# Windowed attention with sinks: both score tiles of a cycle in one run, and the overflow guard from Gram matrices of the weights

## The chip, the cores and the metric

The kernel runs on one core of one Trainium2 chip. The metric is the device time of the whole program in microseconds (us). Before the change three runs took 4219.34, 4223.46 and 4220.33 us; their median is 4220.33 us. The engines are called PE (TensorE, matmuls), PEld (TensorE's weight loads), DVE (VectorE), ACT (ScalarE), POOL (GpSimd) and SP (SyncE, which only starts DMAs here).

## What is computed

The program is a network of 16 stages on 4096 tokens of width 128 (16 sequences of 256). The change lies in one stage, an attention with sinks, whose reference is, cut to its core:

```python
x = rmsnorm(h, attn_norm_scale)
q = apply_interleaved_rope(einsum('bqm,muh->bquh', x, Wq) + bq, cos, sin) * SCALE   # 16 heads of 64
k = apply_interleaved_rope(einsum('bkm,mvh->bkvh', x, Wk) + bk, cos, sin) * SCALE   # 4 heads, SCALE = 64**-0.25
v = einsum('bkm,mvh->bkvh', x, Wv) + bv
scores = einsum('bquh,bkuh->buqk', q, repeat(k, 4))
scores = where(abs(pos[:, None] - pos[None, :]) <= 128, scores, -1e9)
probs = softmax(concatenate([scores, sink], -1))[..., :-1]
h = h + einsum('bquh,uhm->bqm', einsum('buqk,bkuh->bquh', probs, v), Wo) + bo
h = h + moe(rmsnorm(h, moe_norm_scale), ...)
```

The kernel takes the exponential of the scores without subtracting their maximum. So that no overflow can go unseen, it writes bounds into a tile `peaks` as it goes. After the network, `over` (L2759) takes, for each of seven places (`STAGES`, L42), the maximum of the first side times the maximum of the second and compares it with `LIMITS` (L43). If one is above its limit, a second, slower version of the whole network runs. With the inputs given it does not run.

## The kernel before

All activations stay in SBUF, features on the partitions and tokens along the free axis, in eight chunks (`NCH`) of 512 tokens (two sequences of 256). The stage `window` (L2448) holds two buffers of all tokens, `h` and `n1`, calls `window_attention` (L3190), and then the mixture of experts of the same block. It follows the stage `mix` (L2076); the weights of a stage (here `w<-in_window_f`) are loaded while the stage before it runs.

**Units.** The attention's work is cut into 128 units `(c, side, b, it, jt)`: chunk, side (heads 0 to 7 or 8 to 15), sequence in the chunk, tile of 128 queries, tile of 128 keys. Units `n` (even, `jt = 0`) and `n + 1` (odd, `jt = 1`) share their queries. For one unit:

- `score` (L3249): two matmuls of 64 rows of the array each, on the upper and the lower half of the partitions, each 64x128 keys against 512 columns (four heads by 128 queries), into two PSUM banks. ACT then takes the exponential of both into a tile `pt`.
- `masked` (L3262): where `it` and `jt` differ, DVE multiplies `pt` by the window's mask; on the odd unit POOL adds the two units' `pt` into `both`.
- `weigh` (L3272): matmuls with the values as weights, 32 columns each, into the bank `po`; on the odd unit also matmuls of ones with `both`, which give the sums, into the bank `pd`.
- `inverse` (L3296): ACT takes Ln of the sums with the sink added, then Exp of minus that. `divide` (L3304): DVE multiplies `po` by it.

The inputs come from `prepare` (L3226), for a chunk and side in four steps: projections of k and q (`roped`, L3207: one matmul and two DVE operations that read its bank), a shuffle on DVE and an add on POOL (`moved`, L3217), and the values. `before` (L3329) normalises a chunk in three steps: centring, spread, scaling. For chunk 0 its spread is a matmul with the matrix of means; for the later chunks it is the matmuls of L1798 (`compact_spread`), whose rows a DMA spreads out. `after` (L3341) does the second norm likewise. `out` (L3314) is the output projection.

**The order** is written out by hand (`manual_schedule`): each engine runs its instructions as the loop at L3354 emits them. In an even slot n: `score(n)`, then what is due (masks, inverses), then a step of `prepare`, `out`, `before` and `after`, whichever fall there. In an odd slot: `score(n)`, what is due (divides), then `weigh` of units n-3 and n-2. Two slots make a cycle; there are 64 cycles. The slots from -14 to -1 are the ramp: the norm of chunk 0 at -14, -12 and -10, its `prepare` at -8 to -2. Instructions outside the hand-written order (such as `es` and the peak of the sinks at the start of the stage) are placed by the language's scheduler, and may run inside the stage before.

**PSUM** has eight banks; four go by the tag "s" (scores, projections, norms, outputs) and four by "o" (`po` and `pd`, two of each in turn). A bank is used again in the order of the requests for its tag, once its last reader is done.

**The guard.** After each projection `peak` (L1666) takes, on DVE, the largest absolute value of the finished q or k (128x512): 80 of them in the stage. They are due four slots after their `prepare` step.

Of the kernel before, what the change touches and what calls it, by code (L numbers as in the profile page):

```python
# [11 lines left out]
F32, BF16, I32 = mybir.dt.float32, mybir.dt.bfloat16, mybir.dt.int32  # L12
SP = mybir.EngineType.SP
AF = mybir.ActivationFunctionType
ALU = mybir.AluOpType
AX = mybir.AxisListType

P = 128
B, T, C = 16, 256, 128
# [20 lines left out]
BOUND, LOW = 60.0, 38.0  # L40
PEAKS = 4 * NCH
STAGES = DECAY, ROPE, WINDOW, WINDOW1, SINKS, LOCAL_A, LOCAL_B = range(7)  # L42
LIMITS = (BOUND * 8**0.5 / 8, BOUND * 8**0.5 / 4, LOW / 64, LOW / 64, LOW, LOW / 8, LOW / 8)  # L43


class Pack:
# [40 lines left out]
def _rows(v, n=P):  # L87
    v = np.asarray(v)
    return np.broadcast_to(v.reshape(1, -1), (n, v.size))
# [7 lines left out]
def _consts(fast=False):  # L97
# [18 lines left out]
    p.add("ones4", _rows((i[None, :32] // 8 == np.arange(4)[:, None]).reshape(-1)))  # L116
    p.add("limits", [LIMITS[n] for n in STAGES])
    if not fast:
# [1531 lines left out]
class Fast(Net):  # L1650
# [1400 lines left out]
    def guard(self, stage, c, q, k):  # L3051
        self.peak(stage, 0, c, q)
        self.peak(stage, 1, c, k)
# [136 lines left out]
    def window_attention(self, w, h, n1, ns2):  # L3190


        nc = self.nc
        with ExitStack() as st:
            p1 = self.stage(st, "w1", 1)
# [6 lines left out]
            units = [(c, side, b, it, jt) for c in range(NCH) for side in range(2) for b in range(2) for it in range(2) for jt in range(2)]  # L3202
            qs, ks, vs, pts, ots, sums, both, due = {}, {}, {}, {}, {}, {}, {}, {}
# [3 lines left out]
            def roped(n, g, s, t1):  # L3207


                pa = self.bank("s")  # L3210
                self.mm(pa, w["W" + n][:, g * P : g * P + P], n1[:, s])
                t2 = p2.tile([P, CH], F32, tag="t2", name="t2", bufs=4)
                for t, table in ((t2, w["sin"]), (t1, w["cos"])):
                    self.stt(self.bt(t), self.bt(pa), w["b" + n][:, g : g + 1], self.twice(table), ALU.add, ALU.mult)
                pending.append((t1, t2))

            def moved():  # L3217
                t1, t2 = pending.pop(0)
                t3 = p2.tile([P, CH], F32, tag="t3", name="t3")
                nc.vector.stream_shuffle(t3, t2, [d ^ 1 for d in range(32)])  # L3220
                self.gt(t1, t1, t3, ALU.add)

            def later(slot, f, *args):
                due.setdefault(slot, []).append((f, args))

            def prepare(i, step, slot):  # L3226

                c, side = divmod(i, 2)
                s = self.chunk(c)
                while pending:  # L3230
                    moved()
                if step == 0:
                    qs[i] = p2.tile([P, 4, CH], F32, tag="q", name="q")
                    ks[i] = p2.tile([P, CH], F32, tag="k", name="k")
                    roped("k", side, s, ks[i])
                    later(("last", slot + 4), self.peak, WINDOW + side, 1, c, ks[i])
                for g in ((0,), (1, 2), (3,), ())[step]:
                    roped("q", 4 * side + g, s, qs[i][:, g])
                    later(("last", slot + 4), self.peak, WINDOW + side, 0, 4 * c + g, qs[i][:, g])
                if side == 0 and step > 1:  # L3240
                    pv = self.bank("s")
                    v = p1.tile([P, 2, T], F32, tag="v", name="v", bufs=4)
                    for k in range(2):
                        t = 2 * step - 4 + k
                        self.mm(pv[:, k * T : k * T + T], n1[:, c * CH + t * P : c * CH + t * P + P], w["Wv"])
                        vs[c, t] = v[:, k]
                    self.tt(v, self.bt(pv), w["bv"][:, None, :].broadcast_to([P, 2, T]), ALU.add)

            def score(n):  # L3249
                c, side, b, it, jt = units[n]  # L3250
                i0, j0 = b * T + it * P, b * T + jt * P
                q, k = qs[2 * c + side], ks[2 * c + side]
                pt = p2.tile([P, 2, 4, P], F32, tag="pt", name="pt", bufs=6)
                ps = [self.bank("s"), self.bank("s")]
                for half in range(2):
                    rows = slice(64 * half, 64 * half + 64)
                    self.mm(ps[half].rearrange("p (h t) -> p h t", h=4), k[rows, j0 : j0 + P], q[rows, :, i0 : i0 + P])
                for half in range(2):
                    self.act(pt[:, half].rearrange("p h t -> p (h t)"), ps[half], AF.Exp)
                pts[n] = pt  # L3260
# [11 lines left out]
            def weigh(n, slot):  # L3272
                c, side, b, it, jt = units[n]
                if jt == 0:
                    sums[0] = self.bank("o"), self.bank("o")
                pt = pts.pop(n)
                po, pd = sums[0]


                for dh in range(3 if jt else 2):  # L3280
                    if dh == 2:
                        pt = both.pop(n)
                    for r in range(4):
                        half, hh = divmod(r, 2)
                        d = (2 * side + half) * 64 + 32 * dh
                        at = dh % 2 * T
                        nc.tensor.matmul(
                            (pd if dh == 2 else po)[32 * r : 32 * r + 32, at : at + T],
                            self.ones64[:, :32] if dh == 2 else vs[c, 2 * b + jt][:, d : d + 32],
                            pt[:, half, 2 * hh : 2 * hh + 2].rearrange("p h t -> p (h t)"),  # L3290
                            start=dh == 2 or (jt == 0 and dh == 0), stop=dh == 2 or (jt == 1 and dh == 1), skip_group_check=True,
                        )
                if jt:
                    later(slot + 1, inverse, n, po, pd, slot + 2)
# [34 lines left out]
            def before(c, i):  # L3329

                s = self.chunk(c)
                if i == 0:
                    held["sq"] = self.centre_step(p1, self.x[:, s], h[:, s], "s", square=True)
                elif i == 1:
                    held["rs"] = self.spread_step(p1, held["sq"], "s", twice=True, compact=c > 0)
                else:
                    r1, r2 = held["rs"]
                    self.stt(n1[:, s], h[:, s], w["ns1"], r2, ALU.mult, ALU.mult)
                    self.tt(h[:, s], h[:, s], r1, ALU.mult)
# [9 lines left out]
                else:  # L3349
                    self.stt(n1[:, s], h[:, s], ns2, held["rs"], ALU.mult, ALU.mult)  # L3350

            with self.share(s=4, o=4), self.tc.manual_schedule():
                self.logs()
                for n in range(-14, len(units) + 16):  # L3354
                    if 0 <= n < len(units):
                        score(n)
                        later(n + 1, masked, n)
                    for f, args in (*due.pop(n, []), *due.pop(("last", n), [])):
                        f(*args)
                    if n % 2:  # L3360
                        for i in (n - 3, n - 2):
                            if 0 <= i < len(units):
                                weigh(i, n)
                        continue
                    i, step = divmod(n + 8, 8)
                    if 0 <= i < 2 * NCH:
                        prepare(i, step // 2, n)
                    i, rest = divmod(n - 14, 8)
                    if rest == 0 and 0 <= i < 2 * NCH:
                        out(i)  # L3370
                    c, u = divmod(n + 16, 16)
                    if c == 0 and u in (2, 4, 6):
                        before(c, u // 2 - 1)
                    if u in (0, 2, 6) and 0 < c < NCH:
                        before(c, (u + 1) // 3)
                    c, u = divmod(n - 24, 16)
                    if u in (0, 2, 6 if c < NCH - 1 else 4) and 0 <= c < NCH:
                        after(c, (u + 1) // 3 + (u == 4))
# [497 lines left out]
```

## Time and profile before

| what | value |
|---|---|
| median of three runs | 4220.33 us |
| the profiled execution | 4218.15 us |
| its span, first to last instruction | 4216.4 us |
| DVE, pt<-pt,w (mask), 128x1024 | 1.29 us each, one a cycle (2930 to 3300 us) |
| POOL, both<-pt, 128x1024 | 2.36 us each, one a cycle |
| ACT, pt<-ps (exponential), 128x512 | 0.60 us each, four a cycle |
| DVE, t<-ps,w and q<-ps,w (projection), 128x512 | 0.74 to 0.75 us each |
| DVE, peaks<-q, 128x1 from 128x512 | 0.68 us each, 64 in the stage |
| DVE, peaks<-k | 0.67 us each, 16 in the stage |

The profile is of one execution. A row names the engine, the line of the kernel (often a helper's: L504 is every `mm`, L528 every activation), the operation with the tiles that it writes and reads, and how often it stands there. Matmuls of 32-bit numbers appear as two instructions each. A shape such as 64*128 behind a matmul is the part of the array that it takes: rows of the array by columns. "idle before" is time in which the engine did nothing, with the engine and tile that ended it; "issue" is a wait for nothing that the profile shows. In the timeline several like instructions are merged into one row, xN. Since ends of matmuls are modelled, the distance from start to start is the safer reading.

### The profile page before, as it was taken

What the parts mean: (1) busy time and instruction counts of PE and PEld (TensorE: products, weight loads), DVE (VectorE), ACT (ScalarE), POOL (GpSimd) and SP (SyncE); (2) the same over time, 40 slices, a digit from 0 to 9 for tenths busy, and PEclk for the clock granted to TensorE, in tenths of its full rate; (3) what the DMA queues carried; (4) which work ended last, traced back from release to release, by engine and by line L of the source; (5) the groups of instructions that cost most, each with busy time, mean ns of one, the idle gap of its engine ahead of it and who ended that gap; (6) DMA issues with size and microseconds to landing.
All of it is one profiled execution on the core that took longest, in us unless ns stands there. A gap on an engine that the chain in (4) does not pass through costs nothing. (4 is left out here: it accounts for less than half of the span.)

```text
span 4216.4 us, 74153 instructions
## 1 busy us (share of the span) xinstructions
PE 3831.5 (91%) x29030; PEld 2182.7 (52%) x29030; DVE 2551.0 (61%) x4503; ACT 2281.8 (54%) x4478; POOL 1853.7 (44%) x1632
## 2 busy tenths in 40 slices
PE   7999999998899999985989869888999999899978
PEld 3555466464455466454965459543444344455333
DVE  4776576374577477473346633556877676486474
ACT  6665466555766466652457634444554454774532
POOL 4754365232565166225433434454555455321251
PEclk8999999998999999996999979999999999999979
DMA  1800000000000000004920058100000000000000
GB/s 61 347 15 12 11 9 9 22 1 1 20 11 14 6 7 9 6 11 142 323 69 12 17 182 295 41 19 21 16 14 16 8 0 10 7 2 19 6 0 21
DMA packets 110086, 190.88 MB, mean 45 GB/s; under 512 B 16126, under 2 KB 70788, under 8 KB 109600
## 3 DMA queue, kind: packets, MB, share of 16 engines
q1 hardware_dynamic: 97248, 162.83, 11.7%
q0 software_dynamic: 9120, 18.51, 1.3%
q8 instruction: 231, 3.78, 0.4%
q10 hardware_dynamic: 3360, 4.72, 0.3%
q14 instruction: 127, 1.04, 0.1%
HBM read 118.28 MB, written 54.20 MB: 41 GB/s over the span
## 5 line engine op out<-in xcount | busy, mean ns | idle before, releaser
L528 ACT ACTIVATE pt<-ps 128x512 f32<-128x512 f32 x640 | 339.5, 600 | 337.5 <-PE ps L504 336.2
L504 PE MATMUL ps<-hb,w 128*128 128x512 f32 (+1 forms) x960 | 463.7, 617 | 3.9 <-issue 3.3
L504 PE MATMUL ps<-w,hb 128*128 128x512 f32 (+2 forms) x896 | 405.2, 573 | 27.3 <-DVE t L531 18.5
L534 POOL TENSOR_TENSOR t<-t,t 128x512 f32<-128x512 f32 x256 | 319.9, 1271 | 153.7 <-DVE t L531 107.8
L531 DVE TENSOR_TENSOR t<-ps,tab 128x512 f32<-128x512 f32 x512 | 317.5, 681 | 70.1 <-ACT sq L528 66.7
L534 POOL TENSOR_TENSOR t<-t,ss 128x1024 f32<-128x1024 f32 x128 | 243.7, 1904 | 195.2 <-ACT ss L528 194.0
L504 PEld LDWEIGHTS ps<-hb,w 128*128 128x128 f32 (+1 forms) x960 | 179.6, 191 | 261.8 <-issue 220.6
L528 ACT ACTIVATE qkt<-ps 128x512 f32<-128x512 f32 x256 | 140.6, 595 | 299.2 <-PE ps L508 299.2
L531 DVE TENSOR_TENSOR u<-u,ps 128x384 f32<-128x384 f32 (+1 forms) x206 | 121.8, 595 | 277.2 <-ACT u L528 114.9
L534 POOL TENSOR_TENSOR nsq<-ha 128x512 f32<-128x512 f32 x112 | 123.2, 1100 | 354.3 <-ACT ha L528 342.3
L531 DVE TENSOR_TENSOR ot<-ps,rd 128x512 f32<-128x512 f32 (+2 forms) x224 | 143.2, 639 | 209.8 <-ACT rd L528 209.8
L504 PEld LDWEIGHTS ps<-w,hb 128*128 128x128 f32 x896 | 154.1, 193 | 174.4 <-issue 111.7
L534 POOL TENSOR_TENSOR both<-pt 128x1024 f32<-128x1024 f32 x64 | 151.2, 2363 | 199.0 <-DVE pt L531 191.3
L504 PE MATMUL ps<-ot,w 128*128 128x512 f32 x448 | 213.6, 611 | 17.4 <-DVE ot L531 9.9
L504 PE MATMUL ps<-xt,w 128*128 128x128 f32 x1704 | 221.0, 280 | 1.6 <-ACT xt L528 1.5
L2225 POOL DMA_INDIRECT back<-y,x x142 | 139.1, 980 | 186.1 <-ACT y L528 69.5
L504 PE MATMUL ps<-u,w 128*128 128x512 f32 (+1 forms) x448 | 215.4, 605 | 3.4 <-POOL u L534 3.4
L504 PEld LDWEIGHTS ps<-xt,w 128*128 128x128 f32 x1704 | 204.5, 194 | 3.4 <-ACT xt L528 3.4
L528 ACT ACTIVATE u<-ps,w 128x512 f32<-128x512 f32 x160 | 107.7, 685 | 173.3 <-PE ps L504 170.6
L3479 PE MATMUL ps<-qkt 64*128 64x192 f32 (+1 forms) x2048 | 181.8, 311 | 9.6 <-ACT rd L528 9.6
L504 PE MATMUL ps<-ha,w 128*128 128x512 f32 x320 | 176.1, 672 | 11.6 <-ACT f L528 10.2
L504 PE MATMUL ps<-nsq,ct 128*128 128x512 f32 x272 | 154.5, 652 | 30.8 <-POOL nsq L534 26.6
(366 smaller groups left out, 8756.2 us busy)
## 6 DMA issues: line engine op xcount, KB each, us to landing
w<-in_moe_x SPq DMA_DIRECT2D x142, 533.0 KB
rows<-t SPq DMA_DIRECT2D x64, 520.0 KB
nrs<-nrow SPq DMA_DIRECT2D x220, 64.0 KB
x<-rows SPq DMA_DIRECT2D x142, 65.0 KB
w<-in_local_f SPq DMA_DIRECT2D x8, 659.5 KB
y<-back ACTq DMA_DIRECT2D x16, 256.0 KB
y<-back SPq DMA_DIRECT2D x16, 256.0 KB
w<-in_local_f SPq DMA_DIRECT2D x4, 658.5 KB
```

The costliest lines, as they stand in the source:

```text
L504: self.nc.tensor.matmul(out, lhsT, rhs, start=start, stop=stop)
L528: self.nc.scalar.activation(out, in_, func, **kw)
L531: self.nc.vector.tensor_tensor(out, a, b, op)
L534: self.nc.gpsimd.tensor_tensor(out, a, b, op)
L2225: nc.gpsimd.indirect_dma_start(views[i], bass.IndirectOffsetOnAxis(ap=x[:, C : C + 1].bitcast(I32), axis=0), y, None, bounds_check=2 * NT ...
L3479: nc.tensor.matmul(out, kt[rows, g, t * P : t * P + P], qt[rows, g, t * P : t * P + wide], start=(i, t) == (0, 0), stop=i == 1, skip_group ...
```

## The change

Three things are changed in `window_attention`.

1. In the order: `score(n)` and `score(n + 1)` are both emitted in the even slot n, one after the other, and both units' masks are due at n + 2 (before: n + 1 and n + 2). Weighing, inverses and divides keep their slots.
2. The banks: five for "s", two for "o" (`po`), and one with a tag of its own, "d", for `pd`.
3. The guard: the peaks of q and k are gone. Instead POOL makes copies of Wq and Wk scaled by the square of the norm's weights, and twice in the ramp (slots -14 and -12, behind the first and the second step of the norm of chunk 0) a function `guard` makes, for one side, five Gram matrices W^T diag(ns1^2) W of 128x128 and five products of a bias with itself, reduces the rows' absolute sums on DVE, and writes a bound of the squared length of q and k into `peaks`. The limits of both places become (38 x 8)^2, since the bounds are squares.

```diff
@@ -40,7 +40,7 @@
 BOUND, LOW = 60.0, 38.0
 PEAKS = 4 * NCH
 STAGES = DECAY, ROPE, WINDOW, WINDOW1, SINKS, LOCAL_A, LOCAL_B = range(7)
-LIMITS = (BOUND * 8**0.5 / 8, BOUND * 8**0.5 / 4, LOW / 64, LOW / 64, LOW, LOW / 8, LOW / 8)
+LIMITS = (BOUND * 8**0.5 / 8, BOUND * 8**0.5 / 4, (LOW * 8) ** 2, (LOW * 8) ** 2, LOW, LOW / 8, LOW / 8)
 
 
 class Pack:
@@ -3223,6 +3223,30 @@
             def later(slot, f, *args):
                 due.setdefault(slot, []).append((f, args))
 
+            scaled = [p1.tile([P, w["W" + n].shape[1]], F32, tag="s" + n, name="scaled") for n in "qk"]
+            for t, n in zip(scaled, "qk"):
+                nc.gpsimd.tensor_scalar(t, w["W" + n], w["ns1"], w["ns1"], ALU.mult, ALU.mult)
+
+            def guard(side):
+
+                pg, pb = self.bank("s"), self.bank("s")
+                for i in range(5):
+                    k, g = (1, side) if i == 4 else (0, 4 * side + i)
+                    at = slice(g * P, g * P + P)
+                    gram = pb[:, P:T] if k else pg[:, i * P : i * P + P]
+                    self.mm(gram, w["W" + "qk"[k]][:, at], scaled[k][:, at])
+                    b = w["b" + "qk"[k]][:, g : g + 1]
+                    self.mm(pb[:, i : i + 1], b.broadcast_to([P, P]), b)
+                r = p1.tile([P, 5], F32, tag="bound", name="bound")
+                reduce = nc.vector.tensor_reduce
+                reduce(r[:, :4], pg.rearrange("p (m d) -> p m d", d=P), AX.X, ALU.add, apply_absolute_value=True)
+                reduce(r[:, 4:], pb[:, P:T], AX.X, ALU.add, apply_absolute_value=True)
+                self.ts(r, r, P * 16.0 / 15.0, ALU.mult)
+                for k, some in enumerate((slice(0, 4), slice(4, 5))):
+                    at = ((WINDOW + side) * 2 + k) * PEAKS
+                    peaks = self.peaks[:, at : at + some.stop - some.start]
+                    self.stt(peaks, pb[:, some], 16.0, r[:, some], ALU.mult, ALU.add)
+
             def prepare(i, step, slot):
 
                 c, side = divmod(i, 2)
@@ -3233,10 +3257,8 @@
                     qs[i] = p2.tile([P, 4, CH], F32, tag="q", name="q")
                     ks[i] = p2.tile([P, CH], F32, tag="k", name="k")
                     roped("k", side, s, ks[i])
-                    later(("last", slot + 4), self.peak, WINDOW + side, 1, c, ks[i])
                 for g in ((0,), (1, 2), (3,), ())[step]:
                     roped("q", 4 * side + g, s, qs[i][:, g])
-                    later(("last", slot + 4), self.peak, WINDOW + side, 0, 4 * c + g, qs[i][:, g])
                 if side == 0 and step > 1:
                     pv = self.bank("s")
                     v = p1.tile([P, 2, T], F32, tag="v", name="v", bufs=4)
@@ -3272,7 +3294,7 @@
             def weigh(n, slot):
                 c, side, b, it, jt = units[n]
                 if jt == 0:
-                    sums[0] = self.bank("o"), self.bank("o")
+                    sums[0] = self.bank("o"), self.bank("d")
                 pt = pts.pop(n)
                 po, pd = sums[0]
 
@@ -3349,12 +3371,13 @@
                 else:
                     self.stt(n1[:, s], h[:, s], ns2, held["rs"], ALU.mult, ALU.mult)
 
-            with self.share(s=4, o=4), self.tc.manual_schedule():
+            with self.share(s=5, o=2, d=1), self.tc.manual_schedule():
                 self.logs()
                 for n in range(-14, len(units) + 16):
-                    if 0 <= n < len(units):
-                        score(n)
-                        later(n + 1, masked, n)
+                    if n % 2 == 0 and 0 <= n < len(units):
+                        for i in (n, n + 1):
+                            score(i)
+                            later(n + 2, masked, i)
                     for f, args in (*due.pop(n, []), *due.pop(("last", n), [])):
                         f(*args)
                     if n % 2:
@@ -3371,6 +3394,8 @@
                     c, u = divmod(n + 16, 16)
                     if c == 0 and u in (2, 4, 6):
                         before(c, u // 2 - 1)
+                        if u < 6:
+                            guard(u // 2 - 1)
                     if u in (0, 2, 6) and 0 < c < NCH:
                         before(c, (u + 1) // 3)
                     c, u = divmod(n - 24, 16)
```

## The prediction

> **What bounds the kernel now.** I read the page first, then the stage's stretches, then TensorE's timeline in it. The page gives the times and the busiest engine:
>
> ```profile
> span 4216.4 us, 74153 instructions
> PE 3831.5 (91%) x29030; PEld 2182.7 (52%) x29030; DVE 2551.0 (61%) x4503; ACT 2281.8 (54%) x4478; POOL 1853.7 (44%) x1632
> L504 PE MATMUL ps<-xt,w 128*128 128x128 f32 x1704 | 221.0, 280 | 1.6 <-ACT xt L528 1.5
> ```
>
> A share over 16 stages says little about one, so here is this stage by stretches: ramp, ramp, steady work. The columns are the stretch, its length, busy time (instructions) of PE, PEld, DVE, ACT and POOL, the granted clock, and DMA.
>
> ```profile
> 2872.00:2886.00 14.00, 8.58 (x11) 3.12 (x12) 3.81 (x6) 6.42 (x10) 2.15 (x2) 0.67 0.34 119
> 2898.00:2904.00 6.00, 5.41 (x8) 2.02 (x9) 1.97 (x3) 1.09 (x2) 0.54 (x1) 0.50 0.00 0
> 2915.00:3345.00 430.00, 426.88 (x3449) 176.41 (x3448) 341.11 (x539) 214.99 (x491) 240.52 (x138) 1.00 0.06 14
> ```
>
> TensorE is busy 426.88 of 430 us at full clock; DVE has 79%, ACT 50%, POOL 56%. So in the steady part only what shortens TensorE's queue counts, and in the ramp TensorE is not the bound. Two views of TensorE's timeline (start, length, operation):
>
> ```profile
> 3310.62 1.13 PE L504 MATMUL ps<-q,k 64*128 64x512 f32 x4
> 3311.68 3.70 PE L504 MATMUL ps<-ot,w 128*128 128x512 f32 x8
> 3315.31 1.13 PE L504 MATMUL ps<-q,k 64*128 64x512 f32 x4
> 3316.37 1.93 PE L3287 MATMUL ps<-pt,v 128*32 128x256 f32 x32
> 3318.12 0.61 PE L3287 MATMUL ps<-both,ct 128*32 128x256 f32 x8
> 3318.67 1.99 PE L504 MATMUL ps<-q,k 64*128 64x512 f32 x8
> 3320.58 0.64 PE L3287 MATMUL ps<-pt,v 128*32 128x256 f32 x8
> ```
>
> ```profile
> 3103.15 0.43 PE L1798 MATMUL ps<-nsq,ct 128*32 128x128 f32 x8
> 3103.51 1.68 PE L504 MATMUL ps<-q,k 64*128 64x512 f32 x4
> 3105.11 1.93 PE L3287 MATMUL ps<-pt,v 128*32 128x256 f32 x32
> ```
>
> A matmul is two instructions. One cycle (two units) is: scores S, whole-array work P (projections, out), scores S, weighted values and sums W. I read start to start. S alone takes 1.06 (3310.62 to 3311.68, and 3315.31 to 3316.37). Where a cycle has no P, both scores already stand together (x8) and take 1.91, not 2.12. So being split costs 0.20. In the second view, behind the row sums of a norm (R, L1798), S takes 1.60, 0.54 over its 1.06.
>
> **The change, part by part.**
>
> *Both scores in one run.* 64 cycles; in three the scores are together already. 61 x 0.20 = 12.3 us off. All of it is on TensorE's queue, which sets the end.
>
> *The wait behind R.* There are 13 such S; start to start they take 20.0 us where 13 x 1.06 = 13.8. The second half of S waits for one of the four "s" banks, which holds a projection that DVE copies out at 3103.07 to 3103.81. In the new order S stands ahead of the projections and R ahead of W, which takes "o" and "d" banks. When S next needs the projection's bank, all of W (2.3 us) and half of S have passed. Off: 6.2 us. R and W also share the 128*32 shape: a group of sums takes 0.55 where another shape follows (3318.12 to 3318.67) and 0.43 where the same follows (once, at 3339.81). 13 x 0.11 = 1.4 us off.
>
> *Five "s" banks for a run of four.* In cycle order the banks go S S S S P P ...; the sixth taken is the first S bank. The first score half is complete about 1.1 us into the run, and ACT's two exponentials take 1.09 a pair, so the first bank is free at 1.7, while the second P starts at 1.91 + 0.96 = 2.9. [...] By the rows it costs nothing, since the next run comes a cycle later (at least 1.91 + 1.06 + 2.30 = 5.3 us) and ACT needs 2.18 + 1.05 for the inverse in it. [...]
>
> *One "d" bank.* W's sums now wait for the two Ln of the cycle before, and behind them in TensorE's queue stands everything. Ln ends at 1.1 + 2.18 + 0.63 = 3.9 us in the cycle; the sums start at 4.7 in the shortest cycle and about 5.9 in the mean one. Cost 0, margin 0.8.
>
> *No peaks of q and k.* 80 reductions of 0.67 leave DVE (53 us), which is hidden behind TensorE in the steady part. Masks of the earlier unit move half a cycle later, to 1.3 us into the next cycle; POOL's sum of both (2.36) ends at 3.7, before its use at 4.7. Hidden too. In the last cycle it isn't: there DVE first empties the output bank (5.6 us in), then adds, divides and masks, so POOL's sum ends at 11.2 us where it was needed at 9.5 and ended at 9.95 before: +1.3.
>
> *The guard in the ramp.* Twice ten matmuls (20 instructions of 128 weight columns). The page's row above is the nearest: 221.0/1704 = 0.13 us each at full clock, about 0.26 at half: 2.6 to 5.2 us a guard. The first stands in TensorE's queue between the centring (ends about 2876.1) and the mean, which is ready at 2877.51. The second stands behind the mean, and its five DVE operations stand ahead of the scaling of the first chunk. What waits:
>
> ```profile
> 2881.09 0.75 DVE L543 SCALAR_TENSOR_TENSOR hb<-ha,w,nrs 128x512 f32<-128x512 f32 x1 [5.66 <-ACT nrs L528]
> 2881.87 0.69 DVE L531 TENSOR_TENSOR ha<-ha,nrs 128x512 f32<-128x512 f32 x1
> 2884.02 0.75 DVE L543 SCALAR_TENSOR_TENSOR t<-ps,w 128x512 f32<-128x512 f32 x1 [1.46 <-PE ps L504]
> ```
>
> The clock decides. [...] The rows here are slower: work that began at 2881.94 sped up about 2886 (4.4 us), and the run at 2898.59 still had 0.50 to 2904. By the rows some 7 instructions are slow: 3.5 us, to 2879.6, the mean 2.1 late. I take the row. Then: mean 1.0, second guard 2.6, to 2883.2; DVE 0.68 (as 128x16 from 128x512, 682 ns), about 0.3, and three of 0.17: 1.5, to 2884.7. The scaling is late by 3.6 (2.5 with a full clock at once, 8.4 with none). Given back: four reductions of the first k and q lay on DVE's path to the first score (2890.94 to 2892.1 and 2895.28 to 2896.5): 4 x 0.6 = 2.4; first projections at full clock: 1.2 of DVE's waits of 1.46 and 0.30. Net +0.0, ends -1.1 and +6.0.
>
> *The scaled weights on POOL*: 128x1024 took 1.09 (a TENSOR_SCALAR of that shape elsewhere), 128x256 about 0.3. They lie outside the hand-written order; the stage's other such operations ran inside the stage before, at 2826.2 (DVE) and 2873.57 (ACT). Ahead of a POOL step that TensorE waits for (2871.85) it costs up to 1.4; behind the last one (ends 2876.8) it holds the first guard to 2878.2. I take +0.8, ends 0 and 2.1. The first cycles also stall 1.1 us (sums to S 1.67, at 2923.3, while POOL lags); with DVE ahead I take -0.5, ends 0 and -1.1.
>
> Sum: -12.3 - 6.2 - 1.4 + 1.3 + 0.0 + 0.8 - 0.5 = -18.3. Against the profiled execution (4218.15 us; span 4216.4 and 1.75 around it) that is 4199.9; the median of the three runs, 4220.33, is 2.2 higher: **4202.0 us**.
>
> **Rivals.** *The ramp is paid in full*: clock at half through both guards and POOL late: 6.0 + 2.1 for 0.8, so -11: **4209**. For it: 0.67 and 0.50 granted in the ramp. [...] *The single "d" bank* ends on the slow side: place, the sums in W of every cycle; price, what Ln is later than the sums' turn. It decides from about 2.4 us of lateness of ACT in the mean cycle (2.0 margin and 27/64 = 0.42 to lose 27 us); at 0.5 a cycle: 4202 + 32 = **4234**. Against it: ACT waits for TensorE, not the reverse. *The bound is too loose*, the guard fires and the slow network runs as well: from the reference's weights the largest products of bounds are 89.3 x 90.1 = 8,040 against a limit of 92,416, so no.
>
> **How the numbers follow.** As worked out 0.68 (alone 4197 to 4208); the ramp 0.20; the banks 0.07; "d" 0.05. The range of 4195 to 4212 takes in the first two with the bounds of their costs. A measurement can tell about 0.2% (8.4 us) from no change. Faster by more: 0.67 + 0.19 + 0.01 = 0.87; within 0.08 (the banks, and a ramp at its worst); slower 0.05.
>
> **What would show it.** Right: S as x8 of 1.91 in all cycles, no 1.5 to 1.6 behind R, TensorE still over 99% busy in a steady part about 20 us shorter, first score within some us of 2898.6. Wrong: idle time of TensorE before the sums, ended by ACT's rd (the "d" bank); or before S or P, ended by ACT's pt or DVE (the "s" banks); or a first score at 2904 (the ramp). A second network would double the span.

## The result and the profile after

The changed kernel takes 4205.77 us (median of seven runs, 4199.51 to 4210.81). The kernel before, in seven runs on the same chip, takes 4220.33 us. The ratio is 0.9959, with a 95% interval of 0.995 to 0.9969. Measured once more (e9_after below) it is 0.996, interval 0.9947 to 0.9974. So the change saves 14.6 us where 18.3 were forecast.

From the page of the changed kernel:

```profile
span 4205.5 us, 74307 instructions
PE 3817.3 (91%) x29070; PEld 2194.2 (52%) x29070; DVE 2511.1 (60%) x4433; ACT 2279.3 (54%) x4478; POOL 1857.7 (44%) x1634
```

The span is 10.9 us shorter. DVE is 39.9 us less busy (the 80 peaks of q and k are gone), but PE only 14.2. In this execution the stage itself starts 3.69 us later than in the one before (the first chunk's centring at 2878.11 for 2874.42), so fixed stretches of the two spans don't show the same work. I set the same marks side by side instead. The ramp, from the centring to the first score, is in the profile before

```profile
2874.42 1.91 PE L504 MATMUL ps<-x,ct 128*128 128x512 f32 x2
2898.59 2.08 PE L504 MATMUL ps<-q,k 64*128 64x512 f32 x4 [7.64 <-POOL q L534]
```

and after the change, where the centring is at 2878.11,

```profile
2904.43 3.78 PE L504 MATMUL ps<-q,k 64*128 64x512 f32 x8 [6.22 <-POOL q L534]
```

So the ramp is 26.32 us long for 24.17. The steady part, from the first score to the start of the last output projection, before and after (columns as in the prediction):

```profile
2898.59:3344.82 446.23, 443.00 (x3524) 182.08 (x3524) 352.23 (x554) 221.48 (x504) 245.62 (x141) 0.99 0.06 14
2904.43:3334.99 430.56, 424.77 (x3524) 184.59 (x3524) 310.76 (x478) 215.53 (x504) 247.82 (x141) 0.99 0.06 14
```

The same 3524 matmul instructions take 430.56 us for 446.23. TensorE's timeline in one steady cycle shows why:

```profile
3083.25 1.93 PE L3309 MATMUL ps<-pt,v 128*32 128x256 f32 x32
3085.00 0.61 PE L3309 MATMUL ps<-both,ct 128*32 128x256 f32 x8
3085.55 1.99 PE L504 MATMUL ps<-q,k 64*128 64x512 f32 x8
3087.46 3.70 PE L504 MATMUL ps<-ot,w 128*128 128x512 f32 x8
```

The scores are one run of eight instructions, 1.91 us from start to start. They are one run in all 64 cycles; 61 of these take 1.92 us, and three, at half clock in whole or in part, take 3.71, 2.30 and 3.40. Behind the row sums of a norm nothing is waited for any more: R (L1798) starts at 2916.32, the weighted values 0.24 behind it at 2916.56.

**The stage in numbers.** The total scatters by some us from run to run, and the part of it ahead of this stage differed by 15.1 us between two profiled executions on one chip (e1_no_peaks and e3_order_banks), although the code of that part is the same. So I also measure the stage itself, in the timeline, from its own marks: the start of the first chunk's centring (ps<-x,ct), its scaling on DVE (hb), the first score, and the start of the last output projection. Where one kernel was profiled twice, the ramp came out within 0.1 us, and the stage within 0.2 us, except that e7_tail and e9_tail differ by 1.6 (the clock, below). "S" is the sum over all scores, start to start.

| kernel | hb at | first score at | first score to last output | whole stage | S |
|---|---|---|---|---|---|
| before | 6.67 | 24.17 | 446.23 | 470.40 | 143.2 |
| after | 11.44 | 26.32 | 430.56 | 456.88 | 126.4 |
| e1_no_peaks | 5.89 | 21.02 | 445.71 | 466.73 | 143.2 |
| e2_order | 5.89 | 23.39 | 428.11 | 451.50 | 125.0 |
| e3_order_banks | 5.89 | 23.41 | 430.16 | 453.56 | 126.5 |
| e4_split | 11.48 | 26.44 | 439.06 | 465.51 | 136.1 |
| e5_no_guard | 5.88 | 21.03 | 428.01 | 449.04 | 124.9 |
| e6_guard_late | 5.88 | 21.03 | 427.70 | 448.73 | 124.3 |
| e7_tail | 5.89 | 21.04 | 427.04 | 448.09 | 124.4 |
| e8_unscaled | 7.24 | 22.24 | 430.33 | 452.56 | 126.1 |
| e9_after | 11.43 | 26.41 | 430.32 | 456.73 | 126.1 |
| e9_split | 11.48 | 26.45 | 439.08 | 465.52 | 136.1 |
| e9_tail | 5.88 | 21.07 | 425.41 | 446.47 | 123.1 |

Before against after: the ramp costs 2.2 us more, the steady part 15.7 us less, the stage 13.5 us less. From the centring to the last instruction of the program it is 1327.4 us for 1341.9, so 14.6 less, as much as the totals gain. The theory at this point: all of the gain is the order of the scores, and the new guard takes some 5 us of it in the ramp.

### The profile page after: what moved, and what is told of

It is laid out like the page before. It is cut to its first block, busy times and chain, and to the rows that moved or that the text cites. A ratio compares the mean times of both kernels' runs of the same rounds, so it can differ in the third digit from the quotient of the medians.

```text
span 4205.5 us, 74307 instructions
## 1 busy us (share of the span) xinstructions
PE 3817.3 (91%) x29070; PEld 2194.2 (52%) x29070; DVE 2511.1 (60%) x4433; ACT 2279.3 (54%) x4478; POOL 1857.7 (44%) x1634
```

## The experiments

**One part alone: the peaks.** The kernel before without the peaks of q and k (so without any bound for these two places).

```diff
-                    later(("last", slot + 4), self.peak, WINDOW + side, 1, c, ks[i])
...
-                    later(("last", slot + 4), self.peak, WINDOW + side, 0, 4 * c + g, qs[i][:, g])
```

> The kernel before without the 80 reductions of q and k; no bound of this stage is made (that part of the guard is left out). I read two stretches: the ramp, from the start of the first chunk's centring to the first score (24.17 us before, 26.32 after the change), and the steady part, from the first score to the last output projection (446.23 before, 430.56 after). My theory, that the order of the scores gives the gain and the reductions lie behind TensorE: ramp 21.8 (four reductions of 0.6 fewer), steady 445 to 446, time 2 to 3 us less. The rival, that the change gains by relieving VectorE: steady under 440, time 8 us less or more.

Measured: 4177.81 us, ratio 0.9989 (0.9983 to 0.9996). The steady part is nearly unchanged (445.71 for 446.23, S the same 143.2): 53 us of work taken from DVE is worth at most 0.5 us there. In the ramp the first score comes 15.13 us after hb, where before it came 17.50 after.

**One part alone: the order, and the banks with it.** Both keep the peaks and have no new guard.

```diff
-                    if 0 <= n < len(units):
-                        score(n)
-                        later(n + 1, masked, n)
+                    if n % 2 == 0 and 0 <= n < len(units):
+                        for i in (n, n + 1):
+                            score(i)
+                            later(n + 2, masked, i)
```

e3_order_banks has, besides:

```diff
-                    sums[0] = self.bank("o"), self.bank("o")
+                    sums[0] = self.bank("o"), self.bank("d")
...
-            with self.share(s=4, o=4), self.tc.manual_schedule():
+            with self.share(s=5, o=2, d=1), self.tc.manual_schedule():
```

> The kernel before with only the order of scores and masks changed; four banks for the scores and four for the values, reductions of q and k kept. My theory: runs of eight score instructions in every cycle at 1.92 us, no wait behind the row sums; ramp 24.2, steady 431 to 433 (12.3 for the switches, 6.2 for the waits, 1.4 for the shared shape, 1.4 lost at the end); time 12 to 15 less. The rival, that the fifth bank is what makes the order pay: with four banks the next run waits for a projection's bank in most cycles, steady 438 or more, time 8 us less at best.

> The order and the banks (five, two and one) of the change, with the old reductions of q and k in place of the Gram matrices. My theory: ramp 24.2 as before, steady 430 to 432; time 14 to 16 less, 1 to 2 better than the whole change, since the guard's ramp costs more than the reductions do. The rival, that the reductions (53 us of VectorE) would stand in the way of the denser TensorE queue: steady 436 or more.

Measured: e2_order 4162.73 us, ratio 0.9951 (0.9937 to 0.9965); e3_order_banks 4164.24 us, ratio 0.9955 (0.9941 to 0.9968). The order alone takes 18.1 us from the steady part. The banks add nothing to it. By its stage, 451.50 us, the order alone is 5.4 us better than the whole change (456.88): banks and guard, taken together, cost time. The totals, 0.9951 and 0.9959, are too close to show this. TensorE's timeline of e2_order, with four "s" banks:

```profile
2862.11 0.43 PE L1798 MATMUL ps<-nsq,ct 128*32 128x128 f32 x8
2862.35 1.91 PE L3287 MATMUL ps<-pt,v 128*32 128x256 f32 x32
2864.07 0.61 PE L3287 MATMUL ps<-both,ct 128*32 128x256 f32 x8
2864.62 1.99 PE L504 MATMUL ps<-q,k 64*128 64x512 f32 x8
2866.54 1.12 PE L504 MATMUL ps<-hb,w 128*128 128x512 f32 x2
```

No idle time stands before the scores or before the projection behind them. So a run of scores over all four banks does not wait for the exponentials, and the wait behind R goes with the order, without a fifth bank. The 2.0 us by which e3_order_banks is slower in the steady part stand mostly at one place: in it TensorE's clock is halved for 3.4 us from 49.2 us after the centring, and the run of scores there takes 3.6 us; in e2_order the clock is full there and the run takes 1.9.

**The order undone in the changed kernel.** The guard and the five banks stay, the scores stand apart as before.

```diff
-                    if n % 2 == 0 and 0 <= n < len(units):
-                        for i in (n, n + 1):
-                            score(i)
-                            later(n + 2, masked, i)
+                    if 0 <= n < len(units):
+                        score(n)
+                        later(n + 1, masked, n)
```

> The whole change but for the order: scores and masks as before, banks and Gram matrices as changed. My theory: the switches stay, the waits behind the row sums go, since a fifth bank alone avoids them; score runs of four at 1.06 everywhere; ramp 26.3, steady 439 to 441; time 3 to 5 us less. The rival, that the banks give most of it: steady 435 or less. If the waits belong to the order, not to the banks: steady 445 to 446, time 1 us more or the same.

Measured: 4181.38 us, ratio 1.0003 (0.9994 to 1.0011). In the trace the steady part is 7.2 us shorter than before, and 8.5 us longer than with the change. With a fifth bank, even the old order doesn't wait behind R (1.06 from start to start, where it was 1.60):

```profile
2875.92 0.43 PE L1798 MATMUL ps<-nsq,ct 128*32 128x128 f32 x8
2876.28 1.13 PE L504 MATMUL ps<-q,k 64*128 64x512 f32 x4
2877.34 1.93 PE L3309 MATMUL ps<-pt,v 128*32 128x256 f32 x32
2879.09 0.61 PE L3309 MATMUL ps<-both,ct 128*32 128x256 f32 x8
2879.63 1.13 PE L504 MATMUL ps<-q,k 64*128 64x512 f32 x4
2880.69 1.12 PE L504 MATMUL ps<-hb,w 128*128 128x512 f32 x2
```

So the wait behind R can be removed in two ways, by a bank or by the order; the 0.20 us of each split cannot be removed by a bank. The stage is 4.9 us shorter than before, yet the total shows no gain. I come back to that with the last three runs, e9_after, e9_split and e9_tail.

**The guard taken out.** The changed kernel without `guard` and `scaled` (no bound for q and k).

```diff
-            scaled = [p1.tile([P, w["W" + n].shape[1]], F32, tag="s" + n, name="scaled") for n in "qk"]
-            for t, n in zip(scaled, "qk"):
-                nc.gpsimd.tensor_scalar(t, w["W" + n], w["ns1"], w["ns1"], ALU.mult, ALU.mult)
...
-                        if u < 6:
-                            guard(u // 2 - 1)
```

> The whole change without the Gram matrices and the scaled weights; no bound of this stage is made (that part of the guard is left out). Scaling of the first chunk, first score and length of the steady part, each after the change and then as I expect it. My theory, that the guard in the ramp is paid in full and nowhere else: scaling from +11.4 to +5.9 us after the start of the centring (as in the run without reductions), first score from +26.3 to +21.0, steady 428 to 431 as with the change; time 5 less than with the change, ratio to before near 0.994. The rival, that the guard's matmuls pay for themselves by keeping TensorE's clock up: first score at +24 or later, or the steady part 3 us longer.

Measured: 4160.79 us, ratio 0.9955 (0.9941 to 0.9968). The first score comes 5.3 us earlier than in the changed kernel, hb 5.6 us earlier. The rival, that the guard's matmuls pay by keeping the clock up, fails: the steady part is not longer but 2.6 us shorter, since less of it runs at half clock: 4.0 us from the first score on, for 6.1 and then another 3.4 (from 52.9 us after the centring) in the changed kernel.

**Which part of the guard costs.** The changed kernel's timeline in the ramp (start, length, engine, operation, and in brackets the idle time before it):

```profile
2878.11 1.02 PE L504 MATMUL ps<-x,ct 128*128 128x512 f32 x2
...
2879.15 1.26 POOL L534 TENSOR_TENSOR x<-x,r 128x512 f32<-128x512 f32 x1 [2.05 <-DVE r L531]
...
2880.40 1.74 POOL L3228 TENSOR_SCALAR scaled<-w 128x1024 f32<-128x1024 f32 x2
...
2881.65 0.49 PE L504 MATMUL ps<-scaled,w 128*128 128x128 f32 x2 [2.52 <-POOL scaled L3228]
...
2884.51 2.05 PE L504 MATMUL ps<-nsq,ct 128*128 128x512 f32 x2
...
2888.28 0.69 DVE L3242 TENSOR_REDUCE bound<-ps 128x4 f32<-128x512 f32 x1 [2.83 <-PE ps L504]
...
2889.55 0.74 DVE L543 SCALAR_TENSOR_TENSOR hb<-ha,w,nrs 128x512 f32<-128x512 f32 x1
```

POOL makes the scaled weights after its last step of the stage before. TensorE stands 2.52 us in front of the first guard for them, and the mean (ps<-nsq,ct), which needs nothing of the guard, stands behind it in TensorE's queue. It also runs at half clock, 2.05 for the 1.10 us that it takes in the next experiment. That one takes the wait away: the guard multiplies the weights with themselves, so that the norm's weights are left out of the bound.

```diff
-            scaled = [p1.tile([P, w["W" + n].shape[1]], F32, tag="s" + n, name="scaled") for n in "qk"]
-            for t, n in zip(scaled, "qk"):
-                nc.gpsimd.tensor_scalar(t, w["W" + n], w["ns1"], w["ns1"], ALU.mult, ALU.mult)
+            scaled = [w["Wq"], w["Wk"]]
```

> The whole change with the Gram matrices made from the weights themselves instead of the copies scaled on POOL (the norm's weights are left out of the bound). This takes away what the first guard waits for. My theory, that the wait for POOL is one part of the ramp's cost and the matmuls on TensorE's queue the other: scaling from +11.4 to about +9 us, first score from +26.3 to about +24; time 2 to 2.5 less than with the change. The rival, that POOL's copies are all of the cost: scaling at +6.7 or earlier. If they cost nothing: scaling at +11 still.

Measured: 4163.19 us, ratio 0.9959 (0.9945 to 0.9973). TensorE's timeline of it in the ramp:

```profile
2837.95 1.02 PE L504 MATMUL ps<-x,ct 128*128 128x512 f32 x2
2838.96 2.39 PE L504 MATMUL ps<-w 128*128 128x128 f32 x20
2841.21 1.10 PE L504 MATMUL ps<-nsq,ct 128*128 128x512 f32 x2
2842.16 2.29 PE L504 MATMUL ps<-w 128*128 128x128 f32 x20
2846.08 6.15 PE L504 MATMUL ps<-hb,w 128*128 128x512 f32 x10 [1.63 <-DVE hb L543]
```

Now hb comes at 7.24: the guard's matmuls and DVE's reductions together cost 7.24 - 5.88 = 1.4 us, POOL's scaled weights and the half clock that comes with the wait 11.44 - 7.24 = 4.2 us. I had expected about 9; the measured 7.24 lies much nearer to the rival, that POOL's copies are all of the cost.

**The guard where it is hidden.** The same guard, with its matmuls behind the last projections of the ramp (in slot -2, into banks "o" and "d" that nothing uses yet) and its DVE part behind the first scores.

```diff
+            def grams():
+                pb = self.bank("d")
+                for side in range(2):
+                    pg = self.bank("o")
...
+                    if n == -2:
+                        grams()
+                        later(0, guard, 0)
+                        later(0, guard, 1)
...
-                        if u < 6:
-                            guard(u // 2 - 1)
```

> The whole change, with the guard moved: its matmuls stand behind the last projection of the ramp, where TensorE waits some 5 us for the first queries, and write the three banks of the weighing, which are free until then; its VectorE part stands behind the first two scores. My theory: scaling at +5.9, first score at +21 to +22 (40 short matmuls at 0.13 are 5.2 us, about the gap), steady 429 to 432, since VectorE has slack there; time 4 to 5 less than with the change. The rival, that the cost only moves: first score at +24 or later (matmuls at half clock: 10 us in a gap of 5), or steady 433 or more because the first projections of the steady part wait behind the guard's reductions.

Measured: 4164.04 us, ratio 0.9962 (0.9948 to 0.9975). Its first score comes at 21.03, exactly where it is without any guard. The matmuls lie in the idle time in which TensorE waits for POOL's last q:

```profile
2853.26 1.89 PE L504 MATMUL ps<-w,hb 128*128 128x256 f32 x8
2854.99 0.38 PE L504 MATMUL ps<-scaled,w 128*128 128x128 f32 x2
...
2859.23 0.28 PE L504 MATMUL ps<-w 128*128 128x1 f32 x2
2860.87 3.22 PE L504 MATMUL ps<-q,k 64*128 64x512 f32 x8 [1.36 <-POOL q L534]
```

TensorE's wait shrinks from 5.74 us in e5_no_guard to 1.36. By the stage this is 8.1 us better than the change, but behind my last mark 1.5 us of it are lost (the last output projection takes 5.17 us at half clock for 3.70). By the total, 0.9962 against the changed kernel's 0.9959, nothing is shown.

**The tail.** e6_guard_late with the masks of the last pair due at once.

```diff
-                            later(n + 2, masked, i)
+                            if n < len(units) - 2:
+                                later(n + 2, masked, i)
+                            else:
+                                later(n, masked, i)
```

> The same with one more move: the masks of the last two units stand ahead of the last output projection's addition on VectorE. From the last score to the last output projection: 7.82 us before, of which the last score had no output projection ahead of it, 13.96 after the change. My theory: the two waits at the end (0.94 and 0.61 us) go, 12.3 to 12.6; time 1 to 1.5 less than with the guard late. The rival, that the end is set by the chain of the last weighing, inverse, division and projection and not by the mask: 13.5 or more, no gain.

Measured: 4158.57 us, ratio 0.9943 (0.993 to 0.9957). From the last score to the last output projection it takes 13.28 us, where e6_guard_late takes 13.94: 0.66 less, not the 1.4 or more that I had expected. Its timeline at the end:

```profile
3275.66 2.35 POOL L534 TENSOR_TENSOR both<-pt 128x1024 f32<-128x1024 f32 x1 [2.43 <-DVE pt L531]
3276.26 2.83 DVE L531 TENSOR_TENSOR pt<-pt,w 128x1024 f32<-128x1024 f32 x1 [0.77 <-ACT pt L528]
...
3279.26 2.38 POOL L534 TENSOR_TENSOR both<-pt 128x1024 f32<-128x1024 f32 x1 [1.25 <-DVE pt L531]
...
3280.18 2.01 DVE L543 SCALAR_TENSOR_TENSOR hb<-ha,w,nrs 128x512 f32<-128x512 f32 x1
...
3282.84 1.93 PE L3318 MATMUL ps<-pt,v 128*32 128x256 f32 x32 [1.07 <-DVE ot L531]
```

The mask and the scaling take 2.83 and 2.01 us beside POOL's sums, for 1.22 and 0.74 in the changed kernel; and TensorE waits 1.07 us for the divide that stands behind them (it must empty the bank `po`), in place of the waits for the mask and for POOL's sum.

**The totals once more**, on one chip: the changed kernel, e4_split's kernel (e9_split) and e7_tail's kernel (e9_tail).

> The changed kernel again, beside the two others of this call on one chip, so that they can be set against each other directly. Its stage is 13.5 us shorter than that of the kernel before in the profiled execution, so a ratio of 0.9968 if only the stage counts; the measurement of the change gave 0.9959 [0.995, 0.9969]. Theory: between 0.995 and 0.997.

> The changed kernel with the scores of the two units apart again, a second time and in more rounds: its stage was 4.9 us shorter than that of the kernel before, and its total showed no gain (1.0003). Theory, that a stage's length is what counts and the total was scattered by what comes before the stage: 0.9988, and a profiled stage within 1 us of 465.5 us. Rival, that something outside the stage takes the 4.9 us back: again 1.000 with a stage of 465 us. Against the changed kernel on the same chip the theory gives 8.6 us more, the rival 17.

> The changed kernel with the guard behind the last projections of the ramp and the last pair's masks earlier, on the same chip as the changed kernel: stages of 448.1 and 456.9 us, so 8.8 us (0.21%) less than the changed kernel by the stages, a ratio to before near 0.9946. Rival: the stages before and after take the difference back, and it is within 3 us of the changed kernel.

Measured: before 4220.67 us; e9_after 4206.87 us, ratio 0.996 (0.9947 to 0.9974); e9_split 4221.65 us, ratio 0.9997 (0.9986 to 1.0008); e9_tail 4201.32 us, ratio 0.9948 (0.9935 to 0.9962). The stages came out as the first time.

For the split kernel both totals are the rival's number: a stage of 465.5 us, 4.9 us shorter than before, and no gain. One part of this can be seen. The stage is counted to the start of the last output projection, and in both of the split kernel's profiles the clock is halved over that projection. Before, and in e9_split:

```profile
3344.82 3.70 PE L504 MATMUL ps<-ot,w 128*128 128x512 f32 x8 [1.92 <-DVE ot L531]
3347.37 5.40 PE L504 MATMUL ps<-ot,w 128*128 128x512 f32 x8 [1.92 <-DVE ot L531]
```

That is 1.7 us which the table leaves out; all that follows the stage's last mark is 1.0 us longer in the split kernel (872.6 and 872.5 us for 871.6). So 3.9 us should be left of its gain. If they are lost, it is ahead of the stage, where its code is the same; there the trace shows offsets at several places, which are not the same ones in two executions, and single runs of this one kernel reach from 4206 to 4232 us. The interval of the second measurement (0.9986 to 1.0008) still holds the theory's 0.9988, that of the first (0.9994 to 1.0011) does not. I can't tell a cause from scatter there, and it stays open. Against the changed kernel it is 14.8 us slower, between the theory's 8.6 and the rival's 17.

The tail version is 5.6 us faster than the changed kernel on the same chip, of 10.3 us by the stage. Both times its ratio to before was the lowest of the kernels measured with it, but its interval overlaps the changed kernel's, so it is probably the best version, which the totals don't settle.

## Why the prediction was right, step by step

The direction, the mechanism of the gain and the range hold (4205.77, in 4195 to 4212). In the trace the stage gained 13.5 us for a forecast of 18.3. Of the signs that I had named, the runs of eight scores came and the wait behind R went; but TensorE is busy 424.77 of 430.56 us in the steady part, 98.7% and not over 99%, and that part is 15.7 us shorter, not some 20. The terms:

**What bounds it.** Right. Taking the peaks off DVE gives at most 0.5 us in the steady part (e1_no_peaks), and only what shortens TensorE's queue counts.

**Both scores in one run, -12.3, and the wait behind R, -6.2.** Right, and nearly to the size. S fell by 16.8 for 18.5. The difference is clock: in the changed kernel two runs of scores (the first, and the one at 2930.68) take 3.71 and 3.40 us from start to start for 1.92. In e9_tail, where these two run at full clock, S is 123.1, so 20.1 below before, which had slow scores of its own (2.01 us for the first four instructions, at half clock). The split by cause is from e4_split: the fifth bank alone takes 7.1 us off S, the pairing another 9.7. At full clock a split pair takes 2 x 1.059 in e4_split and a joined one 1.917 in the changed kernel, so 0.20 each; the pairs that were split are 60, not 61 (in before the scores stood together in four cycles), which makes 12.1. A cycle with whole-array work now changes the array's shape three times and not four (S, P, W in place of S, P, S, W). Whether the 0.20 us lies in that or in another cost of beginning a run of matmuls, no run here shows.

**R and W of the same shape, -1.4.** Measured -1.6 (the sum over R fell from 5.0 to 3.4).

**Five "s" banks, 0, and the single "d" bank, 0.** Right. The rival of +17 us (4219, the chance of 0.07 on the banks) had the run of scores go at ACT's pace, 2.18 us for 1.91 in each of 64 cycles. That was my estimate, and no run shows it: S is 125.0 us in e2_order and 126.5 in e3_order_banks, for 143.2 before, and in e2_order's timeline a run of scores takes 1.92 us with no idle time before it. The fifth bank isn't needed in the new order at all.

**The tail, +1.3.** Right in mechanism: DVE empties the bank, adds, scales, divides and only then masks, as worked out. In the changed kernel's timeline:

```profile
3322.95 3.70 PE L504 MATMUL ps<-ot,w 128*128 128x512 f32 x8
3326.58 1.93 PE L3309 MATMUL ps<-pt,v 128*32 128x256 f32 x32
3328.34 0.61 PE L3309 MATMUL ps<-both,ct 128*32 128x256 f32 x8
3329.89 1.93 PE L3309 MATMUL ps<-pt,v 128*32 128x256 f32 x32 [0.94 <-DVE pt L531]
3332.43 0.64 PE L3309 MATMUL ps<-both,ct 128*32 128x256 f32 x8 [0.61 <-POOL both L534]
```

The two waits are 0.94 + 0.61 = 1.55 us. The same place before:

```profile
3339.81 0.61 PE L3287 MATMUL ps<-both,ct 128*32 128x256 f32 x8
3340.24 1.91 PE L3287 MATMUL ps<-pt,v 128*32 128x256 f32 x32
3342.26 0.64 PE L3287 MATMUL ps<-both,ct 128*32 128x256 f32 x8
```

From start to start the sums take 1.55 us for 0.43 and the last weighted values 2.54 for 2.02: 1.6 us more, for 1.3. Three more stalls of 0.17 to 0.33 us, together 0.7, stand before the sums of the three cycles ahead; these were not in the forecast.

**The early stall, -0.5.** Wrong in sign. POOL lags behind in the third cycle as it did before, and now it holds up two steps, not one:

```profile
2929.01 0.64 PE L3309 MATMUL ps<-both,ct 128*32 128x256 f32 x8 [1.06 <-POOL both L534]
2930.68 3.47 PE L504 MATMUL ps<-q,k 64*128 64x512 f32 x8 [1.03 <-POOL q L534]
2934.09 2.15 PE L504 MATMUL ps<-hb,w 128*128 128x512 f32 x4
```

The second wait was there before (1.03, at 2924.94); the first is longer by 1.0 than the 0.24 us that the weighted values lost there before (1.99 for 1.75). I had argued from DVE being ahead. But e2_order, which keeps the peaks, has the same two waits (1.02 and 1.03), so they come with the order, and a DVE without the peaks doesn't shorten them. The half clock that follows these waits costs another 1.5 us on the scores.

**The guard in the ramp, 0.0, with the scaled weights, +0.8.** Measured +2.2 for the two (first score at 26.32 for 24.17), and near only because wrong parts cancelled, which is luck. The scaling (hb) is late by 11.44 - 6.67 = 4.8 us, for 3.6 + 0.8 = 4.4. The parts:

- *POOL's scaled weights.* The case "behind the last one" came: the first guard starts 3.5 us behind the centring's start (2881.65 for 2878.11), where the forecast's 2878.2 is 3.8 behind it. But the prediction priced this case at no more than 2.1, and it measures 4.2 (e8_unscaled). Against e8_unscaled, whose first guard starts 1.0 us behind the centring's start, the wait is 2.5; and in the half clock that follows it the first guard takes 0.6 longer (2.86 to the mean for 2.25) and the mean 0.95 (2.05 for 1.10).
- *The guard's own matmuls and reductions.* Put at 3.6, they measure 1.4: without the wait each set of twenty takes 2.3 us, all at full clock. The row (seven slow instructions) was too careful for that case. It also had the work from 2881.94 speed up about 2886; in the profile before, the granted clock is 0.50 to 2887.03 and 1.00 behind it.
- *The credits.* The peaks gave the forecast 2.4 (17.50 less 15.13 from hb to the first score). The full clock for the first projections, put at 1.2, gave 0.25 (14.88 in the changed kernel for 15.13). Not in the forecast was 0.8 that the kernel before lost in its own centring at half clock (hb at 6.67; 5.89 in e1_no_peaks).

So of the 4.8 us by which the stage missed the sum, about 1.4 are the ramp, 1.5 the early stall with its sign turned, 1.0 the tail with the short stalls ahead of it, and most of the rest is the half clock on scores, which I had taken into the ramp and not into the first cycles.

**The rivals.** The ramp paid in full (-11, 4209) went too far: even with POOL late, the ramp cost 2.2. Its 4209 is as near to the measured 4205.77 as my 4202.0, but by chance: what was missing is mostly in the steady part. The banks and the "d" bank fall with e2_order and e3_order_banks.

## What to carry to other kernels

When TensorE is the bound, count how often one shape stands in two short runs in a cycle: joining two of them was worth 0.20 us a cycle here (1.917 us for 2 x 1.059), and the order of the runs also decided whether a bank was free (before, the scores behind R waited for one and took 1.60 us for 1.06; in the new order nothing waits there). A check that nothing waits for should stand in an engine's queue behind the work that others wait for: here the guard put the first score off by 5.3 us in front of the norm's mean (26.32 for 21.03) and not at all behind the last projection (21.03 in e6_guard_late), where TensorE idled anyway. For an operation outside a hand-written order, look up when its engine really finishes what stands ahead of it, since everything behind its reader takes over the delay: here 4.2 us.

## What the runs showed of the hardware

- **Stretches of half clock.** In the profile before, the granted clock in this stage is 0.50 for 3.41 us from 2873.37, for 6.83 from 2880.20 and for 10.24 from 2893.85; in the changed kernel for 3.41 us from 2883.26, from 2890.09 and from 2931.05, and for 10.24 from 2900.32. What was new to me is how little idle time is followed by such a stretch in a running stage: the waits of 1.06 and 1.03 us at 2929 to 2931 in the changed kernel, and of 1.09 and 1.03 in e3_order_banks, where the scores behind them take 3.56 us from start to start. The same two waits in e2_order (1.02 and 1.03) were followed by none: there the clock is 1.00 from 2872 to 2884. Nor were those in e5_no_guard, although the first is longer (1.24 and 1.03, the scores behind them 1.92). So the length of the waits alone does not decide it. What does, no run shows. The price was 2.0 us of the steady part between e2_order and e3_order_banks. Two executions of one kernel (e7_tail, e9_tail) differ by 1.6 in the same way: in the first one the clock is halved for 3.4 us from 21.6 us after the centring, over the first scores, in the second not.
- **The first scores were faster with other matmuls in the idle time ahead of them.** With the guard behind the last projection, the first run of scores took 3.15 us (e6_guard_late) and 1.92 us (e9_tail), for 3.71 in e5_no_guard, which has no guard and has its first score at the same time after the centring. In e5_no_guard the clock is at half for 6.8 us around the first score (from 18.2 us after the centring), in e6_guard_late for 3.4 (from 21.7), in e9_tail not at all. That is a second, unforeseen gain of the later place.
- **DVE beside POOL.** A mask of 128x1024 took 2.83 us beside POOL's sum and 1.22 otherwise; a scaling 2.01 and 0.74 (e7_tail and the changed kernel). In e7_tail the mask ends 1.08 us behind the sum beside it (3279.09 and 3278.01) and the scaling 0.55 us behind its sum (3282.19 and 3281.64), somewhat less than either takes alone (1.22 and 0.74). Why they are slower beside the sum, no run shows.
